# Last FFN beside attention: the two halves of neighbouring token tiles in one order, and its vectors loaded in pieces of 512

## The chip, the core and the metric

The kernel runs on one core of a Trainium2 chip. The metric is the device time of one execution in microseconds (us), lower is better. The engines are TensorE (PE, with its weight loads as PEld), VectorE (DVE), ScalarE (ACT), GpSimd (POOL) and SyncE (SP), which issues the DMAs. Each engine runs its own list of instructions in a fixed order.

## The reference, cut to what matters

Four gated blocks of cross-attention and FFN work on `x` (4 batches, 512 tokens, width 512). The last FFN, the one that is changed, is a ternary-weight FFN of width 2048. It runs once over all tokens:

```python
def activation_quant(x):                       # one scale per token (row)
    scale = 127.0 / clip(max(abs(x), axis=-1), EPS)
    return clip(round(x * scale), -128, 127) / scale
def bitlinear(x, w, b):                        # weights rounded to -1, 0, 1
    return einsum('bsd,fd->bsf', activation_quant(x), weight_quant(w)) + b

h = bitlinear(x, w1, b1)                       # 512 -> 2048
h = gelu(h)
h = layernorm(h, gamma, beta)                  # over the 2048
return bitlinear(h, w2, b2)                    # 2048 -> 512
...
x = x + tanh(g_ffn[3]) * _L3_ffn(_layernorm(x), ...)
```

`b1`, `gamma`, `beta` (2048 each) and `b2` (512) are vectors along the free axis, so on the chip each must be copied to all 128 partitions.

## The kernel before

The 512 tokens of a batch are four tiles of 128 rows. The kernel walks over eight stages, `heads`, one for each batch and half of the network. The last two are `heads[6]` and `heads[7]`: the second half of the network for batches 2 and 3. Each such stage is `f23`: an FFN (`l2f`), then attention with 16 heads (`l3x`). In `l3x` the head's score matmuls are line 788, their maximum on DVE is line 789, the bias made from it line 793, the exponential on ACT line 795, the transposes of the probabilities lines 803 (PE) and 805 (ACT), the product with the values line 961, and the output projection line 979.

The last FFN is `l3f`. For batches 0, 1 and 2 it is written as a generator and laid beside the two `f23` stages; batch 3 is done at the end alone, as the tail (`tail` given, pool `tail`, its four token tiles interleaved by a small clock). Only the order of the work beside attention is a subject here.

How work is laid beside: a list `side` holds generators. Each `yield` of a generator gives a cost. The main work calls `tick(w)` after each of its steps, which adds `w * 0.75` of credit and advances the first generator in `side` until the credit is used up. All instructions written this way get a priority that is 1000 later than the place where they stand:

```python
while q and credit[i] > 0 and not (q is side and waits()):
    tc.cur_priority += behind          # BEHIND = 1000
    try:
        credit[i] -= next(q[0][1])
```

A list scheduler then makes the order of each engine at build time: it takes the instruction of the best priority that is ready in its own model of the chip. What comes out is a fixed list for each engine. A tile of a pool is a slot; an instruction that needs a slot waits until all users of the slot's former tile are done.

`l3f` handles one token tile in `token(t)`, in these steps (costs are the first numbers of the `yield` lines; the second ones are used in the tail alone):

1. Load `x` (tile `xl`, line 1110), statistics (332), layernorm scale (`rsqrt`, 306, on POOL), normalise (1115), quantise (1118 to 1122), transpose (`turned`: PE 1099, ACT 1101).
2. Four slices of 512: matmul with `w1` (1133), scale and add `b1` on DVE (1135), after each pair of slices Gelu on ACT (1138). Costs up to here: 0.7, 0, 1.4, 0.2 and four times 0.7, together 5.1.
3. Mean and variance (1141 to 1153, squares on ACT 1147).
4. Four slices: normalise on ACT (1164), times `gamma` on POOL (1165), plus `beta` on POOL (1166).
5. Maximum of the absolute value on DVE in two halves of 1024 (1169), quantise (1179, 1181), transpose (1099, 1101), 16 matmuls with `w2` into one bank (1187), scale and add `b2` (1190), add to `x` (1191), store (1192). Steps 3 to 5 cost 7.3 together.

The vectors come through the helper `rep` (line 1090), which loads 1024 elements to all partitions (512 KB in SBUF). Beside attention nothing is kept: `b1` is loaded twice for a token tile, but `gamma` and `beta` are loaded anew for each of the four slices, and each of these eight loads brings 1024 elements of which the slice uses 512. `b2` is one load of 512. All of them share the tag `rep` with 3 slots. `xl` has 1 slot, the big tile `Y` (2048 wide) has 2. In the tail `rep` keeps each vector, in a tag of its own.

At the end of `l3f` the four token tiles of a batch are walked one after another:

```python
gens = [token(t) for t in range(NT)]
if not tail:
    for q in gens:
        for cost, _ in q:
            yield cost
```

Of the kernel before, what the change touches and what calls it, by code (L numbers as in the profile page):

```python
# [2 lines left out]

# [6 lines left out]
F32 = mybir.dt.float32  # L10
# [9 lines left out]
ADD, SUB, MUL = ALU.add, ALU.subtract, ALU.mult  # L20
# [34 lines left out]
COPIES_FIRST, COPIES = 200, 60  # L55

FIRST = (0, 1, 2)

GATED = dict(mm=3, acc=3)
ATTEND = dict(mm=3, acc=3)  # L60
# [3 lines left out]
def tile_flamingo(ctx: ExitStack, tc: tile.TileContext, I, out):  # L64
    nc = tc.nc
    v, s, g, pe, sy = nc.vector, nc.scalar, nc.gpsimd, nc.tensor, nc.sync
# [25 lines left out]
    def nm(base):  # L92
        uid[0] += 1
        return f"{base}_{uid[0]}"
# [9 lines left out]
    def accps(name="acc"):  # L104
        return bank("acc", name)
# [87 lines left out]
    for l in range(2):  # L193
        o = l * PAR_MW
        a = cp.tile([128, 64], F32, name=f"nA{l}")
# [3 lines left out]
        c = cp.tile([128, 20], F32, name=f"cw{l}")  # L199
# [15 lines left out]
    def ds_rep(n, c):  # L215

        r = t2()
        sy.dma_start(r, I[n].partition_broadcast(128))
        v.tensor_scalar(r, r, tg[:, c : c + 1], None, op0=MUL)
        return r  # L220
# [422 lines left out]
    def l0f(b, xs, xT):  # L643
        with tc.tile_pool(name=nm("r0"), bufs=4) as rp:
# [41 lines left out]
            for c in range(4):  # L686
                hf, ha = [], []
                for j in range(4):
# [10 lines left out]
                    if c == 1 and j == 0:  # L699
                        acc.update((t, accps()) for t in FIRST)  # L700
                    step()
# [19 lines left out]
    def l1f(b, xs, nxt, zt, yt):  # L721
        xT = ln_T(xs)
        rep = ds_rep("L1_ds", 5)
        acc = {t: accps() for t in FIRST}
        prev, hs = None, []
# [20 lines left out]
    def l2f(b, xs, xT):  # L746
        rep = ds_rep("L2_ds", 6)
        acc = {t: accps() for t in FIRST}
        prev, hs = None, []
# [320 lines left out]

    def l3f(b, lp, ws, ps_of=mbps, tail=None):

        nbuf = {"rep": 3, "Y": 2, "q16": 2, "qT": 1, "yT": 4, "sq": 1, "xl": 1}
        if tail:
            nbuf = {"rep": 1, "Y": 4, "q16": 4, "qT": 2, "yT": 8, "sq": 1}

        def L(tag, shape, dt):
            return lp.tile(shape, dt, tag=tag, name=nm(tag), bufs=nbuf[tag])

        def smallL(n):  # L1080
            return lp.tile([128, n], F32, tag="sm", name=nm("sml"), bufs=32 if tail else 16)

        kept = {}

        def rep(n, f, w=1024):
            if (n, f) in kept:
                return kept[n, f]
            tag = f"rep{n}{f}" if tail else "rep"
            r = lp.tile([128, 1024], F32, tag=tag, name=nm("rep"), bufs=nbuf["rep"])
            sy.dma_start(r[:, :w], I["L3_" + n][w * f : w * f + w].partition_broadcast(128))  # L1090
            if tail:
                kept[n, f] = r[:, :w]
            return r[:, :w]

        def turned(x, tag):

            pb = ps_of("pb").bitcast(BF)[:, :512]
            for k in range(4):
                pe.transpose(pb[:, k * 128 : k * 128 + 128], x[:, k * 128 : k * 128 + 128], ident_b)
            r = L(tag, [128, 512], BF)  # L1100
            s.copy(r, pb)
            return r

        def token(t):

            if tail:
                x = tail[t]
            else:
                x = L("xl", [128, 512], F32)
                sy.dma_start(x, xsc[b * NT + t])  # L1110
            rs, _ = ln_stats([x], smallL)
            yield 0.7, 1.6
            y = L("Y", [128, 2048], F32)
            z = y[:, 0:512]
            s.activation(z, x, AF.Identity, scale=rs[:, 0:1], bias=rs[:, 1:2])
            sc = smallL(8)
            yield 0.0, 0.8
            v.tensor_reduce(sc[:, 4:5], z, AX.X, ALU.max, apply_absolute_value=True)
            act_quant_scale(z, 512, sc[:, 4:5], sc, bl["w1", "mean"])
            v.tensor_scalar(z, z, sc[:, 0:1], MAGIC, op0=MUL, op1=ADD)  # L1120
            zb = L("q16", [128, 512], BF)
            v.tensor_scalar(zb, z, -MAGIC, 127.0, op0=ADD, op1=ALU.min)
            yield 1.4, 2.3
            xq = turned(zb, "qT")
            yield 0.2, 1.2
            m2 = smallL(8)
            for f in range(4):
                c = slice(f * 512, f * 512 + 512)
                if f % 2 == 0:
                    b1r = rep("b1", f // 2)  # L1130
                ps = ps_of("l1")
                for k in range(4):
                    pe.matmul(ps, xq[:, k * 128 : k * 128 + 128], ws["w1", k][:, f], start=k == 0, stop=k == 3)
                r = slice(f % 2 * 512, f % 2 * 512 + 512)
                v.scalar_tensor_tensor(y[:, c], ps, sc[:, 1:2], b1r[:, r], op0=MUL, op1=ADD)
                if f % 2:
                    h = slice((f - 1) * 512, f * 512 + 512)
                    s.activation(y[:, h], y[:, h], AF.Gelu, accum_out=m2[:, f // 2 : f // 2 + 1])
                yield 0.7, 1.1

            v.tensor_tensor(m2[:, 2:3], m2[:, 0:1], m2[:, 1:2], op=ADD)
            v.tensor_scalar(m2[:, 2:3], m2[:, 2:3], -1.0 / 2048, None, op0=MUL)
            yield 0.1, 1.4
            for f in range(4):
                c = slice(f * 512, f * 512 + 512)
                q = L("sq", [128, 512], F32)
                s.activation(q, y[:, c], AF.Square, bias=m2[:, 2:3], accum_out=m2[:, 4 + f : 5 + f])
            yield 0.0, 2.4
            v.tensor_reduce(m2[:, 3:4], m2[:, 4:8], AX.X, ADD)
            v.tensor_scalar(m2[:, 3:4], m2[:, 3:4], 1.0 / 2048, EPS, op0=MUL, op1=ADD)  # L1150
            rsqrt(m2[:, 3:4], 1)
            nms = m2[:, 4:5]
            v.tensor_tensor(nms, m2[:, 2:3], m2[:, 3:4], op=MUL)
            yield 0.1, 0.8
            s2 = smallL(8)
            for f in range(4):
                c = slice(f * 512, f * 512 + 512)
                r = slice(f % 2 * 512, f % 2 * 512 + 512)
                ga, be = rep("gamma", f // 2)[:, r], rep("beta", f // 2)[:, r]
                if tail and f % 2:  # L1160
                    v.scalar_tensor_tensor(y[:, c], y[:, c], m2[:, 2:3], ga, op0=ADD, op1=MUL)
                    v.scalar_tensor_tensor(y[:, c], y[:, c], m2[:, 3:4], be, op0=MUL, op1=ADD)
                else:
                    s.activation(y[:, c], y[:, c], AF.Identity, scale=m2[:, 3:4], bias=nms)
                    g.tensor_tensor(y[:, c], y[:, c], ga, op=MUL)  # L1165
                    g.tensor_tensor(y[:, c], y[:, c], be, op=ADD)
                yield 0.0, 2.2
            for f in range(2):
                v.tensor_reduce(
                    s2[:, 5 + f : 6 + f], y[:, f * 1024 : f * 1024 + 1024], AX.X, ALU.max, apply_absolute_value=True  # L1170
                )
                yield 1.2, 1.2
            v.tensor_tensor(s2[:, 4:5], s2[:, 5:6], s2[:, 6:7], op=ALU.max)
            act_quant_scale(y, 2048, s2[:, 4:5], s2, bl["w2", "mean"])
            yield 0.5, 0.6
            yqs = []
            for f in range(4):
                c = slice(f * 512, f * 512 + 512)
                v.tensor_scalar(y[:, c], y[:, c], s2[:, 0:1], MAGIC, op0=MUL, op1=ADD)
                qb = L("q16", [128, 512], BF)  # L1180
                v.tensor_scalar(qb, y[:, c], -MAGIC, 127.0, op0=ADD, op1=ALU.min)
                yqs.append(turned(qb, "yT"))
                yield 0.7, 0.8
            ps = ps_of("l2")
            for i in range(16):
                f, k = i // 4, i % 4
                pe.matmul(ps, yqs[f][:, k * 128 : k * 128 + 128], ws["w2", f][:, k], start=i == 0, stop=i == 15)  # L1187
            yield 0.0, 4.0
            o = y[:, 0:512]
            v.scalar_tensor_tensor(o, ps, s2[:, 1:2], rep("b2", 0, 512), op0=MUL, op1=ADD)  # L1190
            v.scalar_tensor_tensor(x, o, tg[:, 7:8], x, op0=MUL, op1=ADD)
            sy.dma_start(out[b * NT + t], x)
            yield 1.4, 1.4

        gens = [token(t) for t in range(NT)]
        if not tail:
            for q in gens:
                for cost, _ in q:
                    yield cost
            return  # L1200

        clock = [9.0 * t for t in range(NT)]
        while gens:
            i = min(range(len(gens)), key=lambda j: clock[j])
            try:
                clock[i] += next(gens[i])[1]
            except StopIteration:
                gens.pop(i), clock.pop(i)
# [168 lines left out]
```

## Time and profile before

| what | value |
|---|---|
| three runs | 3795.2, 3807.01, 3809.92 us; median 3807.01 us |
| the profiled execution | 3800.86 us, its span 3799.1 us |
| busy in the span | PE 3154.0 us (83%), DVE 2534.1 (67%), ACT 1950.4 (51%), POOL 1766.8 (47%) |
| `heads[6]` stage, 2780 to 3240 us | PE busy 402.18 of 460 us |
| `heads[7]` stage, 3240 to 3700 us | PE busy 402.94 of 460 us |
| tail, 3700 to 3799 us | PE busy 49.53 of 99 us, DVE 76.44 |

The profile's span is cut from the first to the last instruction; the execution's own time is 1.8 us more. "Busy" counts instructions at work on an engine, without waits. The chain of waits follows back from the last instruction, at each step to what released it.

### The profile page before, as it was taken

How to read it: one execution, taken by the hardware profiler on the slowest of the kernel's cores; microseconds unless marked ns; L12 is line 12 of the kernel's file. 1: busy time of each engine (PE TensorE's matmuls, PEld its weight loads, DVE VectorE, ACT ScalarE, POOL GpSimd, SP SyncE). 2: the span in 40 equal slices, each digit the busy share in tenths (PEclk: the TensorE clock that was granted, in tenths of full speed). 3: DMA queues.
4: the chain of work that ended last, by engine and by line, in shares of the span. 5: the costliest groups of instructions: out<-in, count | busy, mean ns of one | idle time of the engine just before them, and what ended most of it. 6: DMA issues, size and time to landing. Idle time of an engine off the chain costs nothing.

```text
span 3799.1 us, 40541 instructions
## 1 busy us (share of the span) xinstructions
PE 3154.0 (83%) x12216; PEld 1988.0 (52%) x12216; DVE 2534.1 (67%) x4122; ACT 1950.4 (51%) x4357; POOL 1766.8 (47%) x1367
## 2 busy tenths in 40 slices
PE   7796786888967797888898787999989888888985
PEld 3364454554645554555566454576766454655542
DVE  8968676897499878699558888563234445444437
ACT  6464464455441776464544666434326656356544
POOL 5528476676375678467536889000101222112112
PEclk9898897989988899998998899999999999999997
DMA  8676677867665754566767453775565443655310
GB/s 274 221 266 223 207 239 245 279 229 244 202 207 201 253 179 130 195 203 196 259 210 242 146 152 114 234 248 187 186 229 191 141 149 130 206 202 172 122 61 34
DMA packets 316219, 741.37 MB, mean 195 GB/s; under 512 B 33344, under 2 KB 34752, under 8 KB 316000
## 3 DMA queue, kind: packets, MB, share of 16 engines
q1 hardware_dynamic: 316000, 738.78, 58.9%
q8 instruction: 97, 1.59, 0.2%
q14 instruction: 122, 1.00, 0.1%
HBM read 573.69 MB, written 164.95 MB: 194 GB/s over the span
## 4 chain that ended last, share of the span: by engine, by line
PE 22%; POOL 8%; DMA 7%; DVE 6%; issue 6%; ACT 2%; SPq 0%; POOLq 0%; ACTq 0%; DVEq 0%
PE acc L373 3%; POOL y L564 2%; POOL db13x L545 2%; DMA rep<-in_L_beta_dram 2%; PE po L961 2%; PE gate L637 2%; PE gate L638 2%; PE l L1187 1%; PE up L637 1%; PE down L979 1%; PE up L638 1%; PE S L788 1%; DMA out_dram<-xl 1%; DMA rep<-in_L_gamma_dram 1%; POOL Y L1165 1%
## 5 line engine op out<-in xcount | busy, mean ns | idle before, releaser
L544 ACT ACTIVATE mb<-dt,nA 128x512 f32<-128x512 f32 x512 | 349.9, 691 | 426.2 <-DVE db10x L547 62.9
L306 POOL TENSOR_TENSOR sm<-sm,mhalf 128x8 f32<-128x8 f32 (+2 forms) x76 | 130.0, 1711 | 570.0 <-DVE sm L336 231.3
L637 PE MATMUL gate<-xT,w 128*128 128x512 f32 x624 | 282.6, 453 | 79.2 <-ACT fv L896 14.7
L961 PE MATMUL po<-pt,v 128*128 128x512 f32 x512 | 272.7, 631 | 72.1 <-ACT pt L805 71.1
L637 PE MATMUL up<-xT,w 128*128 128x512 f32 x624 | 254.7, 408 | 39.3 <-DVE t L713 33.3
L788 PE MATMUL S<-k,q 128*128 128x512 f32 x512 | 267.9, 623 | 22.8 <-ACT q L946 12.7
L306 POOL TENSOR_TENSOR sml<-sml,mhalf 128x1 f32<-128x1 f32 x32 | 18.5, 579 | 535.0 <-DVE sml L336 245.6
L638 PE MATMUL gate<-xT,w 128*128 128x512 f32 x624 | 259.6, 416 | 4.6 <-DVE xT L240 4.6
L373 PE MATMUL acc<-w,hf 128*128 128x512 f32 x512 | 242.9, 610 | 21.8 <-DVE hf L666 14.6
L795 ACT ACTIVATE P<-S,st,sm 128x512 f32<-128x512 f32 x256 | 199.9, 783 | 117.0 <-DVE st L793 105.0
L638 PE MATMUL up<-xT,w 128*128 128x512 f32 x624 | 252.0, 404 | 0.0
L979 PE MATMUL down<-wo,h 128*128 128x512 f32 x512 | 236.5, 608 | 2.5 <-ACT Q L930 2.2
L789 DVE TENSOR_REDUCE st<-S 128x1 f32<-128x512 f32 x256 | 173.5, 682 | 78.0 <-PE S L788 77.4
L637 PEld LDWEIGHTS gate<-xT,w 128*128 128x128 f32 x624 | 127.4, 204 | 133.1 <-issue 24.2
L803 PEld LDWEIGHTS pT<-ident,P 128*128 128x128 f32 x1024 | 126.4, 143 | 125.4 <-issue 62.9
L961 PEld LDWEIGHTS po<-pt,v 128*128 128x128 f32 x512 | 89.0, 194 | 195.4 <-ACT pt L805 159.5
L805 ACT COPY pt<-pT 128x512 f32<-128x512 f32 x256 | 144.6, 586 | 88.0 <-PE pT L803 87.9
L373 PE MATMUL acc<-w,h 128*128 128x512 f32 x352 | 170.1, 621 | 17.9 <-DVE h L714 10.0
L640 PE MATMUL gate<-xT,w 128*128 128x512 f32 x432 | 180.8, 419 | 4.6 <-POOL w L240 4.6
L803 PE MATMUL pT<-ident,P 128*128 128x128 f32 x1024 | 160.3, 279 | 28.6 <-ACT P L795 20.5
L640 PE MATMUL up<-xT,w 128*128 128x512 f32 x432 | 172.1, 398 | 3.7 <-DVE w L240 3.7
L373 PEld LDWEIGHTS acc<-w,hf 128*128 128x128 f32 x512 | 98.0, 195 | 118.6 <-issue 82.8
(290 smaller groups left out, 9037.1 us busy)
## 6 DMA issues: line engine op xcount, KB each, us to landing
bc<-dbc SPq DMA_DIRECT2D x128, 512.0 KB, 6.0
w<-in_L_d_dram SPq DMA_DIRECT2D x216, 256.0 KB, 3.6
w<-dL_g SPq DMA_DIRECT2D x81, 512.0 KB, 4.6
w<-dL_u SPq DMA_DIRECT2D x81, 512.0 KB, 4.5
rep<-in_L_gamma_dram SPq DMA_DIRECT2D x50, 512.0 KB, 4.6
rep<-in_L_beta_dram SPq DMA_DIRECT2D x50, 512.0 KB, 4.6
w<-dL_q SPq DMA_DIRECT2D x48, 512.0 KB, 5.8
w<-dL_d SPq DMA_DIRECT2D x42, 512.0 KB, 4.5
```

The lines of the kernel that those rows point to most:

```text
L306: g.tensor_tensor(a, a, mhalf[:, :n], op=ALU.pow)
L373: pe.matmul(ps, h[:, c], w, start=first, stop=last)
L544: s.activation(ps, dt, AF.Exp, scale=nA[l][:, d * 16 + n : d * 16 + n + 1])
L637: pe.matmul(ps, wh[:, c], xT[k][:, 0], start=k == 0, stop=False)
L638: pe.matmul(ps, wh[:, c], xT[k][:, 1], start=False, stop=wl is None and k == 3)
L640: pe.matmul(ps, wl[:, c], xT[k][:, 0], start=False, stop=k == 3)
L788: pe.matmul(ps, q[:, c], k, start=True, stop=True)
L789: v.tensor_reduce(st[:, t : t + 1], ps, AX.X, ALU.max, negate=True)
L795: s.activation(p, ps, AF.Exp, scale=r, bias=m, accum_out=st[:, 8 + t : 9 + t])
L803: pe.transpose(ps[:, t * 128 : t * 128 + 128], pt[t][:, kt * 128 : kt * 128 + 128], ident)
L961: pe.matmul(po, vs[kt][:, c], u, start=kt == 0, stop=kt == 3)
L979: pe.matmul(ps, hs[j][:, c], ws[j // 2][:, j % 2], start=j == 0, stop=j == 3)
```

## The change

Beside attention the generator of a token tile gets a mark, `yield HALF, 0.0`, after its four Gelu slices (between steps 2 and 3 above). The walk over the tiles then advances the first half of one tile and the second half of the tile before it in turns, one `yield` of each at a time, and yields the sum of the two costs. The first half has 8 steps, the second 16, so the second runs its last 8 steps alone.

`rep` loads 512 elements instead of 1024. For a token tile that is four loads of `b1`, four of `gamma`, four of `beta` and one of `b2`, each of 256 KB; every slice has its own load. The tag `rep` has 5 slots of 512 instead of 3 of 1024 (10 KB instead of 12 KB a partition), and `xl` has 2 slots instead of 1 (4 KB instead of 2 KB). In the tail the vectors are kept as before, as 13 tiles of 512 instead of 7 of 1024; its order of token tiles is what it was, since the mark costs 0 there.

```diff
+from itertools import zip_longest
+HALF = -1.0
...
-        nbuf = {"rep": 3, "Y": 2, "q16": 2, "qT": 1, "yT": 4, "sq": 1, "xl": 1}
+        nbuf = {"rep": 5, "Y": 2, "q16": 2, "qT": 1, "yT": 4, "sq": 1, "xl": 2}
...
-        def rep(n, f, w=1024):
+        def rep(n, f):
...
-            r = lp.tile([128, 1024], F32, tag=tag, name=nm("rep"), bufs=nbuf["rep"])
-            sy.dma_start(r[:, :w], I["L3_" + n][w * f : w * f + w].partition_broadcast(128))
+            r = lp.tile([128, 512], F32, tag=tag, name=nm("rep"), bufs=nbuf["rep"])
+            sy.dma_start(r, I["L3_" + n][512 * f : 512 * f + 512].partition_broadcast(128))
...
             for f in range(4):
                 c = slice(f * 512, f * 512 + 512)
-                if f % 2 == 0:
-                    b1r = rep("b1", f // 2)
+                b1r = rep("b1", f)
...
-                r = slice(f % 2 * 512, f % 2 * 512 + 512)
-                v.scalar_tensor_tensor(y[:, c], ps, sc[:, 1:2], b1r[:, r], op0=MUL, op1=ADD)
+                v.scalar_tensor_tensor(y[:, c], ps, sc[:, 1:2], b1r, op0=MUL, op1=ADD)
...
                 yield 0.7, 1.1
+            yield HALF, 0.0
...
-                ga, be = rep("gamma", f // 2)[:, r], rep("beta", f // 2)[:, r]
+                ga, be = rep("gamma", f), rep("beta", f)
...
         if not tail:
-            for q in gens:
-                for cost, _ in q:
-                    yield cost
+            old = iter(())
+            for q in gens + [iter(())]:
+                new = iter(lambda: next(q, (HALF, 0.0))[0], HALF)
+                for a, c in zip_longest(new, old, fillvalue=0.0):
+                    yield a + c
+                old = (c for c, _ in q)
             return
```

More of the change, by code (lines that the diff above doesn't have):

```diff
@@ L1088, in rep @@
             tag = f"rep{n}{f}" if tail else "rep"
-            r = lp.tile([128, 1024], F32, tag=tag, name=nm("rep"), bufs=nbuf["rep"])
-            sy.dma_start(r[:, :w], I["L3_" + n][w * f : w * f + w].partition_broadcast(128))
+            r = lp.tile([128, 512], F32, tag=tag, name=nm("rep"), bufs=nbuf["rep"])
+            sy.dma_start(r, I["L3_" + n][512 * f : 512 * f + 512].partition_broadcast(128))
             if tail:
-                kept[n, f] = r[:, :w]
-            return r[:, :w]
+                kept[n, f] = r
+            return r
         def turned(x, tag):
@@ L1157, in token @@
                 c = slice(f * 512, f * 512 + 512)
-                r = slice(f % 2 * 512, f % 2 * 512 + 512)
-                ga, be = rep("gamma", f // 2)[:, r], rep("beta", f // 2)[:, r]
+                ga, be = rep("gamma", f), rep("beta", f)
                 if tail and f % 2:
@@ L1189, in token @@
             o = y[:, 0:512]
-            v.scalar_tensor_tensor(o, ps, s2[:, 1:2], rep("b2", 0, 512), op0=MUL, op1=ADD)
+            v.scalar_tensor_tensor(o, ps, s2[:, 1:2], rep("b2", 0), op0=MUL, op1=ADD)
             v.scalar_tensor_tensor(x, o, tg[:, 7:8], x, op0=MUL, op1=ADD)
```

## The prediction

> **What bounds the kernel now.** I read the page first (PE is busiest, 83%), then the windows of the two stages, then the waits of each engine between 2870 and 3700 us, where the twelve token tiles run, then the chain of waits, then DVE, ACT and PE instruction by instruction at one of the waits.
>
> In 2870 to 3700 us PE is busy 728.86 of 830 us, so 101 us are idle: the most that any order can win. Where does the idle time lie? Over 41 windows of 20 us from 2880, the 15 in which POOL is busy over 5 us (its multiplications by gamma and additions of beta) have 3.47 us of PE idle each, the other 26 have 1.79. Attention without that step runs nearly full:
>
> ```profile
> core 0: us, PE busy (x) PEld busy (x) DVE busy (x) ACT busy (x) POOL busy (x), PEclk, DMA share, GB/s
> 2900.00:2940.00 40.00, 39.80 (x203) 24.68 (x201) 12.03 (x28) 25.48 (x65) 3.45 (x2) 1.00 0.25 86
> 3560.00:3640.00 80.00, 78.29 (x351) 45.95 (x352) 29.76 (x70) 41.56 (x104) 3.85 (x3) 0.98 0.19 64
> ```
>
> The largest wait of DVE in this stretch is for that POOL step, and POOL itself waits for its vectors (columns: who waited for whom, total us, times, longest):
>
> ```profile
> DVE sml L1169 <- POOL Y L1166: 91.9, 24, 7.3
> POOL Y L1166 <- DMA rep<-in_L_beta_dram: 31.5, 26, 3.0
> DVE sml L332 <- DMA xl<-xsc: 25.5, 11, 4.8
> PE pb L1099 <- DVE q L1181: 20.4, 7, 4.5
> POOL Y L1165 <- DMA rep<-in_L_gamma_dram: 14.7, 14, 1.8
> PE pb L1099 <- DVE q L1122: 6.0, 4, 2.4
> ```
>
> How such a wait reaches PE is seen in the timelines of DVE, ACT and PE (start, length; in brackets the idle time before it and its cause):
>
> ```profile
> 2980.13 0.68 DVE L789 TENSOR_REDUCE st<-S 128x1 f32<-128x512 f32 x1
> 2985.61 1.22 DVE L1169 TENSOR_REDUCE sml<-Y 128x1 f32<-128x1024 f32 x1 [4.80 <-POOL Y L1166]
> ...
> 2987.41 0.20 DVE L793 TENSOR_SCALAR st<-st,sm 128x1 f32<-128x1 f32 x1
> 2987.65 0.78 ACT L795 ACTIVATE P<-S,st,sm 128x512 f32<-128x512 f32 x1 [5.65 <-DVE st L793]
> 2988.58 0.47 PE L803 MATMUL pT<-ident,P 128*128 128x128 f32 x1 [4.28 <-ACT P L795]
> ```
>
> The FFN's maximum (1169) stands in DVE's list ahead of attention's bias (793). While it waits 4.80 us for POOL, the exponential waits 5.65 and PE 4.28. So the FFN costs its own PE time and these holes. The chain of waits shows why POOL is late:
>
> ```profile
> 2973.54 4.56 DMA rep<-in_L_gamma_dram
> 2978.23 1.28 POOL Y L1165
> 2979.53 4.66 DMA rep<-in_L_beta_dram
> 2984.32 1.27 POOL Y L1166
> ...
> 3002.89 4.36 DMA out_dram<-xl
> 3007.32 2.71 DMA xl<-xsc
> ```
>
> Two loads of 512 KB lie bare in one POOL step of 14.7 us (2970.91 to 2985.61) that holds 8 x 1.27 = 10.2 us of work. And each tile starts only when the former one is stored, 7 us, since `xl` has one slot.
>
> **The change part by part.** The sum is made against the profiled execution, 3800.86 us (span 3799.1); the median of the three runs, 3807.01, is 6.15 higher, and I add that at the end. About 0.5% (19 us) is what a measurement of this kernel can tell from no change.
>
> *Price of a DVE wait.* The excess idle of the POOL windows is 15 x (3.47 - 1.79) = 25.2 us for 91.9 us of DVE wait: 0.27 us of PE per us on average (0.9 in the case above).
>
> *Gamma and beta in pieces, 5 slots.* 96 loads of 512 KB, median 4.5 us, become 96 of 256 KB; the nearest row of that kind, `b2` (256 KB, also to all partitions), has 3.8 us. With five slots, two slices and one more vector are at hand when POOL starts, and a slot comes free every 1.27 us while a load takes 3.8 plus 0.33 of issue. POOL has 3 x 1.27 = 3.8 us of other work in that time, so its 46.2 us of DMA waits (31.5 + 14.7) should nearly go. They are half of DVE's 91.9: 0.5 x 25.2 = 12.7 us of PE. The other half is POOL's own work, and I leave it. PE's 20.4 us before the transposes (1099) for line 1181 stand behind the same late maximum; half: 10.2 us. Bounds: nothing (POOL is late anyway) to 25.2 + 20.4 = 45.6.
>
> *Two `xl` slots.* DVE's 25.5 us for `xl` go, since the next tile can be loaded long before: 25.5 x 0.27 = 7.0 us (0 to 25.5 x 0.9 = 23).
>
> *b1 in pieces.* 24 loads of 512 KB become 48 of 256 KB, SP issues 13 loads for a tile instead of 11. Issue is 0.33 us, and SP spends hundreds of us in this stretch on waits for slots (129.6 us for line 1135 alone), so that is hidden; without that cover it costs 24 x 0.33 = 8 us. What is queued behind on SP are attention's `k`, `v`, `w` and `wo`: no PE wait of this stretch ends on a DMA now. In transfer time, b1 goes from 2 x 4.6 = 9.2 to 4 x 3.8 = 15.2 us for a tile, +72 us in all, against 96 x 0.7 = 67 saved on gamma and beta. They run far ahead of use, so I take 0; wholly bare it is 72 x 0.27 = 19 us. The Trainium skill ("DMA: Bandwidth & Descriptors", Rules for kernel authors) says to coalesce many small transfers, which speaks against splitting. The trace agrees in rate (256 KB in 3.8 us is 69 GB/s, 512 KB in 4.6 is 114), but half of each gamma and beta load is never used. By the rule alone the gain below would shrink by those 19 us to 11.
>
> *The two halves in turns.* The same instructions, the same sum of costs (12.4 a tile). The first half's PE, DVE and ACT work (8 steps) stands beside the second half's mean, gamma and beta steps. DVE and POOL so work at the same time more often: POOL's step takes 1.27 us in this stretch (DVE busy 45%) and 1.47 and 1.38 in the tail (DVE busy 77%). 96 x 0.15 = 15 us of POOL, at 0.27 +4 us at most; DVE's load stays nearer to the first row, so 0. In "SBUF — State Buffer", Who interferes with whom, the Trainium skill gives a reason for such rows: a DVE instruction with two SBUF inputs and a reading GpSimd instruction exclude each other. By it the sum would be those 4 us worse. A Gelu costs ACT a table load; beside attention there are 11 to Gelu and 11 back, one pair a tile, 1.28 us each. Should the new order double them, 22 x 1.28 = 28 us of ACT, which is busy 458 of 830 us; at 0.27, 8 us. I take 0. That a tile is done sooner, some 40 us a tile instead of 65, brings nothing by itself while PE sets the pace.
>
> *Tail.* 13 issues of SP instead of 7, the same bytes; the first b1 piece lands 0.8 us sooner, the last vector some 2 us later, under other work: 0 (-1 to +2).
>
> Sum: 12.7 + 10.2 + 7.0 = 29.9, say 30 us: 3771 for a profiled execution, 3777 as a median.
>
> **The rivals.**
>
> *The tiles themselves were the bound.* For: the chain of waits goes along the token tiles from 2871 to 3663 us almost unbroken, and loads and stores of theirs are a fifth of it. Then all DVE waits for POOL and `xl` and all of PE's waits for 1099 go: 25.2 + 26.4 + 23 = 75 at most, which leaves 26 of the 101 us idle; two or three quarters of it, 60: 3747. Against: PE is 88% busy, and many of its holes (21 us at the change of stage, lines 356, 637 and 606) are not the tiles'.
>
> *No change.* The order is planned anew; POOL's 10.2 us a tile stay, DVE still stands at 1169, and attention's own waits (PE for 805: 22.0 us, for 795: 14.7) take up what is freed. Also if the planner keeps the halves one after another, since the tiles stand 1000 later than attention: then only the loads count. About 3807.
>
> *Slower: the shared ring.* The loads now stand in the order gamma, beta, b1 of the next tile, gamma, beta, b1. A b1 piece holds its slot until PE and DVE have done the next tile's matmul, which has low priority. If the four matmul slices of a tile spread over more than the 14.7 us that POOL's step takes, gamma and beta are left with one or two slots, and each of the last three slices then waits about 4.1 - 2.5 = 1.6 us for its vectors, and up to 20 us for one stuck b1 piece. With 5 us more of DVE wait a tile, 12 x 5 = 60 us, PE loses between 16 (0.27) and 54 (0.9): 36 in the middle, 3843. For: SP waits 129.6 us for slots held by b1 now. Against: the two Gelus of a tile, which mark the ends of slices 2 and 4, start 1.5 to 5.9 us apart in eleven tiles and 13.3 in one, so the slices rarely spread that far.
>
> **How the numbers follow.** The forecast (3762 to 3792) 0.40, of which 0.04 lie within 0.5%; tiles the bound 0.13; no change 0.20, of which 0.03 slower; shared ring 0.27, of which 0.02 within. Faster 0.36 + 0.13 = 0.49; same 0.04 + 0.17 + 0.02 = 0.23; slower 0.03 + 0.25 = 0.28. The range goes from the most that the holes allow, 3807 - 75 = 3732, to a little past the slower rival, 3846; what lies outside is its worse part and more than all the holes. By the forecast alone it is 3762 to 3792.
>
> **What would show it.** Right: POOL's waits for gamma and beta below 15 us, DVE's wait at 1169 near 45, no DVE wait for `xl`, PE's wait before 1099 near 15, PE idle in the stretch near 70. Wrong: a DVE wait at 1169 as long as now with POOL never waiting for a DMA (POOL's own time decides); longer waits of POOL for `rep` with SP standing at line 1135 (the shared ring); PE waits for `k`, `v` or `w`; or the same holes at 805 and 795 although 1169 is quick (attention's own).

## The result and the profile after

| | before | changed |
|---|---|---|
| median of six runs each | 3803.95 us (3795.2 to 3816.15) | 3767.69 us (3759.45 to 3772.49) |
| ratio | | 0.9902, 95% interval 0.988 to 0.9925 |
| profiled execution (span) | 3800.86 us (3799.1) | 3769.34 us (3767.6) |

The median fell by 36 us; the forecast was 30. The tail is as long as it was (the last matmul of attention's projection starts at 3697.9 us of 3799.1 before and at 3667.2 of 3767.6 now, 101 and 100 us from the end), so the whole gain lies beside attention. From 2870 us to the end of attention PE is idle 797 - 724 = 73 us instead of 101, in this row of the windows of the changed kernel (the prediction said "near 70"):

```profile
core 0: us, PE busy (x) PEld busy (x) DVE busy (x) ACT busy (x) POOL busy (x), PEclk, DMA share, GB/s
2870.00:3667.00 797.00, 723.98 (x3256) 437.25 (x3257) 374.92 (x889) 473.55 (x1083) 169.93 (x142) 0.95 0.40 125
```

The waits of the changed kernel (line numbers are 2 to 4 higher: the maximum is 1171, POOL's two steps 1167 and 1168, the statistics of `x` 335, the transposes 1103, the first matmuls 1136, the `b1` addition 1137):

```profile
DVE sml L335 <- DMA xl<-xsc: 37.5, 7, 11.0
POOL Y L1167 <- DMA rep<-in_L_gamma_dram: 28.4, 13, 6.8
DVE sml L1171 <- POOL Y L1168: 20.2, 7, 5.5
POOL Y L1168 <- DMA rep<-in_L_beta_dram: 17.8, 18, 3.8
PE pb L1103 <- DVE q L1126: 15.6, 4, 6.8
PE pb L1103 <- DVE q L1183: 3.9, 3, 2.5
```

Read against the rows of before, this is not the picture that was forecast. DVE's wait at the maximum fell from 91.9 to 20.2 us, further than the 45 expected. But POOL waits for gamma and beta as long in total as before, 28.4 + 17.8 = 46.2 us, and DVE waits longer for `x` than before, 37.5 instead of 25.5. PE's own waits before the transposes moved in the same way: behind the maximum (for line 1183, 1181 before) they fell from 20.4 to 3.9 us, behind the quantising of `x` (line 1126, 1122 before) they grew from 6.0 to 15.6.

Why the maximum no longer waits is seen in DVE's timeline for the first tile. POOL finished that tile's last addition at 2901.41 us:

```profile
2928.80 0.75 DVE L1137 SCALAR_TENSOR_TENSOR Y<-l,sml,rep 128x512 f32<-128x512 f32 x1 [5.22 <-PE l L1136]
...
2935.94 0.74 DVE L1137 SCALAR_TENSOR_TENSOR Y<-l,sml,rep 128x512 f32<-128x512 f32 x1
2936.60 1.21 DVE L1171 TENSOR_REDUCE sml<-Y 128x1 f32<-128x1024 f32 x1
...
2938.32 0.74 DVE L1137 SCALAR_TENSOR_TENSOR Y<-l,sml,rep 128x512 f32<-128x512 f32 x1
...
2940.54 0.74 DVE L1137 SCALAR_TENSOR_TENSOR Y<-l,sml,rep 128x512 f32<-128x512 f32 x1
2941.20 1.21 DVE L1171 TENSOR_REDUCE sml<-Y 128x1 f32<-128x1024 f32 x1
```

The two maxima now stand between the neighbour's `b1` additions, 35 us behind POOL. Those additions wait for PE, which is harmless: while DVE waits for PE, PE is working. Of the seven waits that are left, six are of the last tile of each batch, which has no neighbour; the seventh is 1.73 us.

The new hole is the load of `x`. SP's timeline, then DVE's and PE's, at the third tile:

```profile
2973.32 0.34 SPq L1194 DMA_DIRECT2D out_dram<-xl  x1
2977.04 2.55 SPq L1094 DMA_DIRECT2D rep<-in_L_b_dram  x2
2979.68 0.38 SPq L1114 DMA_DIRECT2D xl<-xsc  x1
```

```profile
2984.14 0.69 DVE L335 BATCH_NORM_STATS2 sml<-xl 128x6 f32<-128x512 f32 x1 [7.63 <-DMA xl<-xsc]
...
2989.30 0.43 DVE L1126 TENSOR_SCALAR q<-Y 128x512 bf16<-128x512 f32 x1
2989.78 0.61 PE L1103 MATMUL pb<-ident_b,q 128*128 128x128 bf16 x4 [6.76 <-DVE q L1126]
```

The third tile's load stands behind the store of the first (2973.32): with two slots, and two tiles under way, the slot comes free only then. DVE stands 7.63 us, PE 6.76.

### The profile page after: what moved, and what is told of

It is laid out like the page before. It is cut to its first block, busy times and chain, and to the rows that moved or that the text cites. A ratio compares the mean times of both kernels' runs of the same rounds, so it can differ in the third digit from the quotient of the medians.

```text
span 3767.6 us, 40618 instructions
## 1 busy us (share of the span) xinstructions
PE 3143.5 (83%) x12216; PEld 1989.1 (53%) x12216; DVE 2540.2 (67%) x4122; ACT 1963.8 (52%) x4369; POOL 1763.7 (47%) x1367
## 4 chain that ended last, share of the span: by engine, by line
PE 25%; POOL 7%; DVE 6%; DMA 5%; issue 4%; ACT 3%; SPq 0%; POOLq 0%; ACTq 0%; DVEq 0%
PE acc L376 3%; PE po L964 2%; PE down L982 2%; POOL y L567 2%; PE S L791 2%; POOL db13x L548 1%; PE gate L640 1%; PE gate L641 1%; PE up L641 1%; PE up L640 1%; PE l L1189 1%; PE pT L806 1%; POOL db12x L548 1%; POOL Y L1167 1%; PE gate L643 1%
## 5 line engine op out<-in xcount | busy, mean ns | idle before, releaser
L640 PE MATMUL gate<-xT,w 128*128 128x512 f32 x624 | 280.7, 450 | 69.9 <-ACT fv L899 14.4
L312 PE MATMUL Q<-w,xT 128*128 128x256 f32 x512 | 156.7, 306 | 7.0 <-DVE xT L243 7.0
```

The costliest lines, as they stand in the source:

```text
L312: pe.matmul(ps, lh, rh, start=start, stop=False)
L640: pe.matmul(ps, wh[:, c], xT[k][:, 0], start=k == 0, stop=False)
```

## Experiments

All were timed against the kernel before on the same chip. The chips differ, though: the medians of the kernel before lie between 3798.55 and 3803.95 us, so a gain is best read from the ratio. "Waits" are DVE's for POOL at the maximum plus those for `x`; "PE idle" is from 2780 us to the end of attention. Both come from one profiled execution of each kernel.

| kernel | median us | ratio (95%) | waits us | PE idle us |
|---|---|---|---|---|
| before | 3804 | 1 | 91.9 + 25.5 | 114 |
| before_b950 | 3799.32 | 0.9993 (0.9982 to 1.0004) | 98.2 + 22.7 | 107 |
| pieces | 3793.53 | 0.9984 (0.9972 to 0.9996) | 94.0 + 13.5 | 102 |
| pieces_xl2 | 3802.54 | 1.001 (0.9999 to 1.0022) | 80.9 + 0 | 103 |
| spread | 3795.43 | 0.9981 (0.997 to 0.9991) | 82.1 + 23.6 | 105 |
| before_nobeta | 3764.67 | 0.9901 (0.9887 to 0.9916) | 55.8 + 19.0 | 81 |
| before_dve | 3772.31 | 0.9924 (0.991 to 0.9938) | 11.4 + 14.4 | 85 |
| turns | 3763.03 | 0.9907 (0.9888 to 0.9926) | 59.8 + 26.6 | 73 |
| changed | 3767.69 | 0.9902 (0.988 to 0.9925) | 20.2 + 37.5 | 85 |
| after_b950 | 3782.15 | 0.9949 (0.9935 to 0.9964) | 19.1 + 43.4 | 89 |
| xl3 | 3737.3 | 0.9839 (0.9817 to 0.9861) | 22.5 + 0.7 | 54 |
| after_nobeta | 3726.63 | 0.9798 (0.9785 to 0.9811) | 9.3 + 20.9 | 55 |
| chain | 3722.52 | 0.9794 (0.978 to 0.9807) | 13.9 + 0 | 53 |
| chain_dve | 3725.91 | 0.9804 (0.9791 to 0.9817) | 4.7 + 0 | 53 |

### Which part of the change gains

**pieces**: the loads alone.

```diff
 # changed kernel, with the walk of before and one xl slot (lines cut)
-"xl": 2
+"xl": 1
...
-for q in gens + [iter(())]: ... zip_longest(new, old) ...
+for q in gens:
+    for cost, _ in q:
+        if cost != HALF: yield cost
```

> The loads alone: 512 in 5 slots, the token tiles one after another as before, one xl slot. The theory of the recorded prediction (smaller loads spare POOL its waits for gamma and beta, and so DVE its wait at the maximum) expects 23 of the 36 us: about 3781 us, POOL's waits for rep below 15 us, DVE's wait at the maximum near 46. The rival (the order in turns puts other work of DVE ahead of the maximum; the loads matter little, since POOL waits 46 us for them in the changed kernel too) expects 3795 to 3810 us and DVE's wait at the maximum at 60 us or more.

Measured 0.9984, some 6 us, where the prediction's theory expected 23. The forecast's first half came true: POOL's waits for `rep` are gone altogether, no row of them is left. Its second half did not:

```profile
DVE sml L1171 <- POOL Y L1168: 94.0, 24, 7.8
DVE sml L335 <- DMA xl<-xsc: 13.5, 11, 2.4
```

DVE waits at the maximum as long as before. POOL is done sooner, but the maximum stands as close behind it in DVE's list as ever. Inferred, not shown: the planner puts it where its own model has POOL done, and the model follows the shorter loads too.

**turns**: the order in turns with two `xl` slots, the loads as before.

```diff
 # changed kernel, beside attention (lines cut): b1 twice a tile, gamma and beta anew for each slice
-"rep": 5
+"rep": 3
...
+r = lp.tile([128, 1024], F32, tag="rep", ...)
```

> The order in turns and two xl slots, but beside attention the loads stay as they were: 1024 wide, 3 slots (the tail keeps its pieces of 512). The theory of the order expects most of the gain, 3765 to 3785 us, with DVE's wait at the maximum at 15 to 40 us. The theory of the loads expects 3795 us or more, since three slots are now shared by two tiles and POOL's waits for rep grow past 46 us.

Measured 0.9907, the whole gain of the change. POOL's waits for its loads became far longer, and the gain was there all the same:

```profile
POOL Y L1178 <- DMA rep<-in_L_gamma_dram: 72.1, 29, 5.6
POOL Y L1179 <- DMA rep<-in_L_beta_dram: 70.9, 31, 4.6
DVE sml L1182 <- POOL Y L1179: 59.8, 12, 10.3
DVE sml L335 <- DMA xl<-xsc: 26.6, 8, 6.0
```

POOL waits 143 us for its vectors, three times as long as before, and the kernel is 35 us faster. So the order, with its second `xl` slot, is the part that gains, and no gain of the pieces on top of it can be measured. DVE's wait at the maximum was 59.8 us, above the 40 that the theory of the order allowed: that theory named the right part but not the whole mechanism. The changed kernel has 29 us less of these waits than turns, but 12 us more PE idle and the same time (at a granted clock of 0.923 against 0.920, see below), so the gain of the order does not come from the wait at the maximum alone; what else it comes from is open.

**pieces_xl2**: as pieces, with two `xl` slots.

> The loads in pieces and two xl slots, the token tiles one after another. In this order the second slot lets the next tile's x be loaded while the former tile runs. The recorded prediction's step for xl expects DVE's 25.5 us of wait for xl to go and 7 us (up to 23) less than with the pieces alone. If tiles ahead of time are worth nothing because PE sets the pace, it is the pieces' time within 5 us.

DVE's wait for `x` went to 0 and the time did not fall: 1.001, against 0.9984 for the pieces. PE idle is the same, 103 and 102 us. So no gain of the second slot alone is seen in the old order, where the waits for `x` were 1.2 us on average (13.5 in 11, in the pieces). That the median is even 9 us above that of the pieces goes with a lower granted clock, as shown under "What another order is worth by itself".

**xl3**: the changed kernel with `"xl": 3`.

> The changed kernel with three xl slots instead of two. In the changed kernel DVE waits 37.5 us for xl, up to 11.0 at once, and PE stood 6.76 us behind one such wait of 7.63. Reason supposed: the first half of a tile starts in the round after the tile two before it is stored, so with two slots its load still stands behind that store. With three slots the wait should fall below 10 us, and 28 us of DVE wait at 0.27 to 0.9 give 8 to 25 us: 3743 to 3760 us. The rival (SP's list is late for other reasons, a load of b1 or b2 that waits for a slot stands ahead of it) expects the wait to stay over 25 us and the time within 5 us of 3768.

```profile
DVE sml L1171 <- POOL Y L1168: 22.5, 8, 6.1
DVE sml L335 <- DMA xl<-xsc: 0.7, 1, 0.7
```

Median 3737.3 us: 24 us less than the changed kernel by the ratios, 30 by the medians, a little more than expected, and PE idle falls from 85 to 54 us. In the new order these waits were 5.4 us on average, up to 11.0, and PE paid 31 us for 37 of them, 0.8 a us. The rival, that SP's list is late for other reasons, is out: the wait is gone. The Trainium skill ("DMA: Bandwidth & Descriptors", Rules for kernel authors) says to issue a DMA early and wait for it late, so that its fixed cost overlaps; this pair of runs agrees with it, one slot of 2 KB for 24 to 30 us.

### What the maximum's wait is worth

**spread**: before, with the costs of the second half moved.

```diff
-                yield 0.0, 2.2      # after each gamma and beta slice
+                yield 0.7, 2.2
-                yield 1.2, 1.2      # after each maximum
+                yield 0.05, 1.2
-            yield 0.5, 0.6
+            yield 0.0, 0.6
```

> The kernel before with its order, loads and slots; only the costs of the second half are moved: each of the four gamma and beta slices yields 0.7 instead of 0, the two maxima 0.05 instead of 1.2 and the quantise scale 0 instead of 0.5 (the sum stays 12.4). So the maximum is written down about one head of attention later than POOL's step, in place of right behind it. Theory of the distance (the order in turns gains because it puts the maximum far behind POOL's step in DVE's list, whatever stands between): DVE's wait at the maximum falls from 92 to below 35 us and the time to 3765 to 3785 us. Theory of the other tile (what gains is that the neighbour's first half stands in the gaps of the second): time 3793 to 3805 us.

Inconclusive on the theory, since the edit did not do what it was made for: the maximum was not moved. In the second tile POOL's multiplications start at 2980 to 2991 us and the maxima at 2986 and 2995, as close as before. So a later place in the program did not by itself move the maximum back in DVE's list; that the neighbour's additions do so in the changed kernel is read from its timeline above, and no run here separates the distance from the other tile's work.

**before_nobeta** and **after_nobeta**: without the loads and additions of beta beside attention.

> The kernel before without loads and additions of beta beside attention (the tail keeps them): POOL's step is 5.1 us a tile instead of 10.2. If DVE's wait for POOL is what costs, the wait falls from 92 to 30 to 50 us and the time by 10 to 25 us, to 3775 to 3790. If what costs lies elsewhere, since the planner puts the maximum right behind POOL's step in any case, the wait stays over 60 us and the time within 8 us of 3800.

> The changed kernel without loads and additions of beta beside attention. POOL's step no longer stands ahead of DVE there (its wait is 20.2 us), so a shorter step should bring at most 6 us directly; SP has 48 loads fewer, and if the loads of the ring keep x waiting (37.5 us), part of that goes too: 3745 to 3768 us. A theory in which POOL's step still sets the pace of the tiles expects 3740 us or less.

Before: 37 us less for 43 us less wait (36 of them at the maximum, 91.9 to 55.8), more gain than expected. Changed kernel: 41 us less, which the expectation gave to the theory that POOL's step still sets the pace. But DVE's waits fell there as well, from 57.7 to 30.2, more than half of it for `x` (37.5 to 20.9), presumably because SP has 48 loads fewer ahead of it. Both kernels also have less work. These two runs alone can't tell the causes apart.

**before_dve** and **chain_dve**: the second and fourth slice of gamma and beta on DVE, nothing left out.

```diff
-                if tail and f % 2:
+                if f % 2:
```

> The kernel before, with the second and fourth slice of gamma and beta done on DVE beside attention too (two instructions of 0.75 us a slice, as in the tail) instead of ACT and POOL: POOL's step is 5.1 us a tile shorter, DVE has 36 us more work in all, nothing is left out. If DVE's waits for POOL and for x are what holds PE up (117 us before; over nine kernels some 0.6 to 1 us of time for each us of them), they fall to 75 to 90 and the time to 3765 to 3785 us. If the run without beta gained by its missing loads or work, or DVE's own load matters more, 3795 us or above.

> The turns with three xl slots and batches 0 and 1 in one row (3722 us), with the second and fourth slice of gamma and beta on DVE as in the tail. DVE's waits for POOL and x are only 13.9 us there, so the theory of these waits expects at most 10 us less: 3712 to 3724 us. If POOL's step sets the pace of the tiles whatever DVE waits for, as much as in the runs without beta (37 to 41 us): 3680 to 3695 us.

Before: the wait at the maximum falls from 91.9 to 11.4 us and the time by 0.76%, 29 us, with 36 us more work on DVE. But DVE now multiplies by gamma and adds beta itself, and so waits itself for these loads, which the column "waits" does not hold (the first two rows are before_dve's, the others chain_dve's):

```profile
DVE Y L1161 <- DMA rep<-in_L_gamma_dram: 36.6, 17, 4.6
DVE Y L1162 <- DMA rep<-in_L_beta_dram: 23.5, 19, 3.1
DVE Y L1163 <- DMA rep<-in_L_gamma_dram: 27.3, 10, 7.3
DVE Y L1164 <- DMA rep<-in_L_beta_dram: 18.2, 15, 3.4
```

With them DVE's waits fall from 117.4 to 11.4 + 14.4 + 60.1 = 85.9 us, 31.5 us for 29 us of time. So waits of DVE cost time also with the work complete, though POOL's shorter step and ACT's shorter list changed in the same run. In the kernel whose waits are nearly gone already (13.9 us), the same edit brings nothing (3725.91 against 3722.52), with PE idle at 53 us in both. POOL's step is 5.1 us a tile shorter there, but 45.5 us of new DVE waits stand against it; so whether POOL's step sets the pace by itself is not shown.

**chain**: xl3, with batches 0 and 1 in one row of eight tiles, so that the fourth tile has a neighbour too.

```diff
-gens = [token(t) for t in range(NT)]
+gens = [token(b, t) for b in bs for t in range(NT)]
...
-for b in range(2):
-    side.append(((b,), l3f(b, lp, ws3)))
+side.append(((1,), l3f((0, 1), lp, ws3)))
```

> The changed kernel with three xl slots, and batches 0 and 1 walked as one row of eight tiles, so that the last tile of batch 0 also has a neighbour; with three slots alone 3737 us. In that kernel 3 of the 12 tiles have none, and DVE's 22.5 us of wait at the maximum are theirs. Theory of the distance: tile 4's share, some 7 us of DVE wait, goes, and 2 to 6 us of time: 3731 to 3736. Rival (PE is nearly full, 54 us of holes are left, and they are at the changes of stage): within 4 us of 3737.

3722.52, 15 us below xl3, more than the 2 to 6 expected: 0.9794 of before, the fastest version here. In the profiled executions the two are closer, 5 us apart (3723.16 and 3728.42, the latter 9 us under xl3's median), and PE idle differs by 1 us (53 and 54), so 10 of the 15 us are not in these traces. The other three runs of xl3 had a lower granted clock (0.919 to 0.921) than those of chain (0.922 to 0.926), which would be enough for it by the estimate in the next part.

### What another order is worth by itself

**before_b950** and **after_b950**: `BEHIND = 950` instead of 1000.

> The kernel before, planned anew and nothing else: the side work's priority is 950 later instead of 1000. It measures what another order of the lists is worth by itself. Expected: within 10 us of 3802, DVE's waits for POOL and x within 15 us of 117.

> The changed kernel with the side work's priority 950 later instead of 1000, the same control: within 10 us of 3768, DVE's waits for POOL and x within 15 us of 58. If the change gained by a lucky order, the time goes back towards 3800.

The kernel before stays where it was. The changed one loses half of its gain, 0.9949 against 0.9902, which is 19 us instead of 37 and more than the 10 us expected. DVE's waits are not the reason (62.5 us against 57.7). The first rows of the two pages, the changed kernel and then after_b950, show where the time went:

```profile
PE 3143.5 (83%) x12216; PEld 1989.1 (53%) x12216; DVE 2540.2 (67%) x4122; ACT 1963.8 (52%) x4369; POOL 1763.7 (47%) x1367
PE 3174.3 (84%) x12216; PEld 2006.5 (53%) x12216; DVE 2541.5 (67%) x4122; ACT 1958.4 (52%) x4365; POOL 1766.7 (47%) x1367
```

The same 12216 matmuls took 31 us longer, while PE was idle 9 us less over the span (614.9 us against 624.1). The mean granted clock of PE, the share of full speed at which it was let run, was 0.913 in this execution and 0.923 in the other, and busy time times clock comes to nearly the same, 2898 and 2901 us; in all fourteen profiles it lies between 2898 and 2914. All six runs of after_b950 had a clock of 0.913 to 0.919, those of the changed kernel 0.920 to 0.924. pieces_xl2 is a second such case: its twelve runs had 0.915 to 0.919, those of the pieces 0.917 to 0.924, 0.004 apart on average. From PE's 3160 us that is an estimated 3160 x 0.004 / 0.92 = 14 us, enough for the 9 by which it is slower. Why these orders are granted a lower clock is not shown. So half of the measured gain can hang on how the lists happen to fall; a gain of 19 us remains in both orders.

## Why the prediction was right, point by point

The sign, the size (36 against 30) and the idle time of PE (73 against 70) came out; the terms of the sum did not. That the sum came so near is luck: the terms that made up its 30 us are worth 6 us (the pieces) and nothing seen (the slot) by themselves, and the term put at 0 brought the gain.

- *What bounds the kernel*: right as far as the runs show. PE's holes beside attention were the thing to win, and DVE's waits make many of them: over the fourteen kernels PE's idle time falls with them, from 117 us of waits with 114 idle to 14 with 53. It is no strict rule: turns has 86 with 73, the changed kernel 58 with 85, pieces_xl2 81 with 103. One reading was too strong: in the POOL step of 14.7 us POOL stood idle for 4.5 us in all, so the two loads "bare" in it, 9.2 us long, ran for the most part beside POOL's work.
- *Gamma and beta in pieces* (12.7 + 10.2 us): this step failed. That POOL's waits for DMA go was right for the loads alone; that half of DVE's wait goes with them was wrong: 94.0 us stayed. The loads are worth 6 us in the old order. In the changed kernel POOL's waits are back at 46.2 us, in a ring now shared with the next tile's `b1`, as the slower rival had it, but without its harm: DVE seldom stands behind POOL any more.
- *Two xl slots* (7.0): failed twice. DVE's wait for `x` grew to 37.5 us, because I took it that the next tile could be loaded long ahead; in turns, the slot comes free only when the tile two before is stored. And in the old order, where the wait did go, no gain of the slot is seen.
- *The two halves in turns* (0): mis-sized. With the second slot, it is the whole gain, 35 us by the run with the old loads. I had counted its instructions and costs, which do not change, and not what it puts between POOL's step and the maximum.
- *Price of a DVE wait* (0.27): too low. From the runs it is 0.8 (xl3), 0.9 (before_nobeta, 37 for 43, with work left out), 0.9 (before_dve, 29 for 31.5, with more work on DVE), and nothing seen for waits of 1 us (pieces_xl2). So the sum came near by a price too low on waits that changed otherwise than forecast.
- *b1 in pieces* (0): right. 256 KB take 3.4 to 4.0 us to land by the medians, near the row of `b2` (3.8); the 19 us that wholly bare transfers would have cost are not seen (pieces: 6 us less).
- *DVE and POOL side by side* (0): right; POOL's steps take 1.29 us instead of 1.27, 96 x 0.02 = 2 us.
- *Table loads* (0): they went the feared way, from 11 pairs to 17. The first timeline above shows how: other work stands between two additions of `b1`, and so between a tile's two Gelus. The 12 loads more are 15 us of ACT, and what they cost in time was not measured by itself.
- *Tiles the bound*: not shown. In every one of these kernels the last tile's store is issued within 6 us of the end of attention, which fits both readings. Against it, taking the wait for `x` out of the tiles' chain (pieces_xl2) left PE as idle as it was; for it, the run after_nobeta gained some 40 us for 27.5 us less wait, though with work left out.

## What to carry to other kernels

Where an engine's list is fixed, look at what stands behind an instruction that waits for a slower engine, not only at how to make the slower engine sooner: here DVE's maximum held up attention, and laying the neighbour's ready work beside that half of the tile was worth all of the gain, while sparing POOL its loads was worth a sixth of it by itself. When two tiles are put under way at once, count the slots again for both: one slot of 2 KB too few cost 24 to 30 us, nearly as much as the change brought. Replan without a change once (a priority moved a little) before reading a difference below half a per cent, and read the granted clock beside the waits: here another order of the same work was granted 0.5% less clock and lost half the gain.

## What was not expected of the hardware

A load of an activation table stood in the way for its own 1.28 us only. In the kernel before, ACT's load at 3019.24 us follows the read that ended at 3019.22, and the Gelu starts at 3020.53. It is the same at the other loads up to 3700 us in the kernel before and in the changed one, 57 in all: each starts within 0.03 us of the end of the instruction before it, and in the 38 cases where ACT then waits for no other engine, the next instruction starts within 0.06 us. The Trainium skill ("ScalarE: Activation LUTs", What ACT_TABLE_LOAD costs) gives 1283 ns for the load, which every such row here agrees with, and a drain of about 1380 ns on top of it, which these places do not show.
